# Another order of the attention and feed-forward stages in the second layer of a fused transformer kernel

## The chip, the core and the metric

One core of a Trainium2 chip. TensorE (PE) multiplies, its weight loads (PEld) overlap with its products; VectorE (DVE), ScalarE (ACT) and GpSimd (POOL) work element by element; SyncE (SP) issues the DMAs. The metric is the time of one execution on the device in microseconds; lower is better. A measurement here is the median of three executions.

## What is computed

A causal single-head attention with residual and layer norm (the front), then a block of two transformer layers with windowed attention, then a last residual and layer norm. Cut to what matters, for 8 sequences of 1024 tokens and 256 channels:

```python
x = layernorm(x + attn(x))                    # front: one head, causal
y = x
for l in range(2):                            # DEPTH
    h = shift_token(y)                        # second half of the channels from the token before
    q, k, v = split(h @ wqkv[l])              # 8 heads of 64
    q, k = rotary(l2norm(q) * qs[l], l2norm(k) * ks[l])
    # windows of 128 tokens: each looks at itself and the one before
    o = softmax(mask(8 * q @ k.T)) @ v
    y = y + o @ wo[l]
    h = layernorm(shift_token(y)) * lg[l] + lb[l]
    a, g = split(h @ w1[l] + b1[l])           # 682 hidden
    y = y + (a * gelu(g)) @ w2[l] + b2[l]
x = layernorm(x + y)
```

All of it is float32. Weight products run as three products of fp32r halves (high x high, high x low, low x high), which the helper `products` lists.

## The kernel before

`fronts` computes the front for all sequences and leaves x in DRAM (`x0_d`). `layers` then does both layers; the first leaves its result in `x1_d`. The unit of work is a window of 128 tokens; a pair of windows (256 tokens) shares one transposed input and one pass of the feed-forward. There are 2 x 8 x 8 = 128 windows and 64 pairs, 32 pairs for each layer.

The stages of a window, in `attention`:

- `prep` (once for a pair): load x, transpose it on PE (`l_xp`), write high and low halves (`l_xT`)
- `qk` (t, k), k = 0, 1: six products of 512 columns into `l_pqk`, which hold q and k of four heads; squares on ACT and sums on DVE (`l_ss`, L757), two products with the rotary tables on DVE (`l_t`, L764), two sums on POOL (L771)
- `v`: six products of 512 columns (`l_pv`), copied by ACT to `l_v`
- `unit`: inverse norms with POOL's power (L142, L144), and k scaled by them (L782)
- `turn` (t, k): four transpositions (`l_t` on PE), high half by ACT, low half by DVE into `ring`, which keeps three windows
- `sc` (w, u), u = 0, 1: scores of four heads, 12 products over 64 rows each; mask and row minimum on DVE (L843), exp on ACT (L703) into `l_e`. With u = 1 come the reciprocals of the sums (`rd`, L855), their transposition, a way through DRAM (`rd_d`, L860) and back spread over the partitions (`l_R`, L866)
- `et` (w, u): eight transpositions of `l_e` on PE, two ACT copies to `l_eT` (L885). Window 0 of a sequence has four, since it has no window before it
- `val` (w, u): 16 value products, each to 64 of the output's partitions, into one `l_po` per window
- `out`: `l_po` times `l_R` on DVE (`l_on`, L909), high half by ACT (L914), low half by POOL (L915)
- `proj`: 12 products with `wo` (`l_py`), added to x by DVE (L927). After an odd window the pair's feed-forward is put in a queue.

The feed-forward is a generator of 11 steps, one for each `side`: (1) the shifted copy `m_sh` by DMA (L947, L948), statistics on DVE (L152, L153), POOL's power (L144), `m_hn` on DVE (L964); (2) four transpositions `m_hp` and the halves `m_hT`; (3 to 8) `m_pag` for six chunks of the hidden size, 12 products of 256 columns, six for the last chunk, with gelu on ACT (L703), bias and product on DVE (L1013), halves by DVE (L1016) and POOL (L1017); (9, 10) `m_pf`, 17 products each; (11) the sum on DVE (L1043), in the second layer also the last norm (`o_st`, `o_mv`, L1052), and the store.

The order is written out by hand. `ORDER` is one round, for windows w and w + 1 with w = 2j; an entry such as `("sc", -2, 0)` means the stage `sc` of window w - 2 with u = 0. There are 11 `side` entries in a round, one pass of the feed-forward. The framework's scheduler puts the instructions into each engine's queue by priority and readiness. For PE the order is bound further by `queued` (a group's products are those with `part=True`, scores and values): all other products ahead of a group in the program come before it, and all behind it after it. Within a queue an instruction that waits holds up what stands behind it.

PSUM has eight banks: four `ps` buffers for everything but scores, and four `sc` buffers. In SBUF `l_eT` and `l_oT` have two buffers each, `l_v` four, `l_t` six, `x` six. `table` keeps ACT's exp and gelu from being mixed, since either needs its own table to be loaded.

Of the kernel before, what the change touches and what calls it, by code (L numbers as in the profile page):

```python
# [26 lines left out]
def kernel(  # L27
# [141 lines left out]
    for j, s in ((0, 1), (1, -1), (2, 1)):  # L169
        nc.gpsimd.affine_select(  # L170
            out=mask[:, j, :], in_=mask[:, j, :], compare_op=ALU.is_ge, fill=FAR,
# [38 lines left out]
    def q4(shape, name, dt):  # L210
        return qpool.tile(shape, dt, tag="q4", name=name, bufs=QB)

# [270 lines left out]
    def load_qkv(l, stage, W):  # L483

        wqk = pair([P, 2, 2, 2, INNER // 2], "wqk", wpool)
        wvv = pair([P, 2, INNER], "wvv", wpool)
        for c in range(2):
            for k in range(3):
                st = stage([P, INNER], f"st_qkv_{l}_{c}_{k}")
                nc.sync.dma_start(  # L490
                    out=st, in_=wqkv[l, c * P : (c + 1) * P, k * INNER : (k + 1) * INNER]
                )
                if k < 2:
                    s3 = st.rearrange("p (g f) -> p g f", g=2)
                    split_weight(wqk[0][:, c, :, k, :], wqk[1][:, c, :, k, :], s3)
                else:
                    split_weight(wvv[0][:, c, :], wvv[1][:, c, :], st)
                yield
        W["wqk"] = [t.rearrange("p c g k f -> p c (g k f)") for t in wqk]
        W["wv"] = wvv  # L500

    def load_wo(l, stage, W):
        W["wo"] = pair([P, INNER // P, E], "wo", wpool)
        for c in range(0, INNER // P, 2):
            st = stage([P, 2, E], f"st_wo_{l}_{c}")
            nc.sync.dma_start(
                out=st, in_=wo[l, c * P : (c + 2) * P, :].rearrange("(c p) e -> p c e", p=P)
            )
            split_weight(W["wo"][0][:, c : c + 2, :], W["wo"][1][:, c : c + 2, :], st)
            yield  # L510
# [52 lines left out]
    def load_b1(l, stage, ps, W):  # L563
        b1_tiles(l, W)
        for c in range(2):
            pb = ps(f"pb1_{l}_{c}")
            for k, m0, m1, st in w1_parts(l, stage, c):
                b1_part(W, pb, c, k, m0, m1, st)
            b1_add(W, pb)
            yield  # L570
# [37 lines left out]
    def load_w2(l, stage, W):  # L608
# [23 lines left out]
        yield  # L632

    QB = 4
    PSB = {"ps": 4, "sc": 4}
    ORDER = [
        ("qk", 0, 0), ("unit", -2), ("unit", -1), ("side", 1), ("turn", -2, 0), ("side", 1),
# [3 lines left out]
        ("v", 0), ("side", 1), ("prep", 2), ("v", 1), ("et", -2, 1), ("et", -1, 0),  # L641
        ("val", -2, 0), ("val", -2, 1), ("et", -1, 1), ("side", 1), ("qk", 1, 1),
        ("val", -1, 0), ("val", -1, 1), ("side", 1), ("side", 1), ("side", 1),
    ]

    def layers(pool, psum):
# [14 lines left out]
        def ps(name):  # L661
            return psum.tile([P, 512], FP, tag="ps", name=name, bufs=PSB["ps"])

        def ps_sc(name):
            return psum.tile([P, 2, 256], FP, tag="sc", name=name, bufs=PSB["sc"])

# [393 lines left out]
        def side(n):  # L1060
            for _ in range(n):
                if not queue:
                    return
                try:
                    next(queue[0])
                except StopIteration:
                    queue.pop(0)
# [3 lines left out]
        def run(name, w, *args):  # L1071

            if not 0 <= w < DEPTH * B * NT:
                return
            l, b, t = w // (B * NT), w // NT % B, w % NT
            if (l, b) not in A:
                if "wqk" not in Ws[l]:
                    for _ in load_qkv(l, stage, Ws[l]):
                        pass
                W = Ws[l]  # L1080

                def finished(p, xt):
                    queue.append(feed_forward(l, b, p, xt, W))

                A[l, b] = attention(l, b, W, finished)
            A[l, b][name](t // 2 if name == "prep" else t, *args)
            if name == "proj" and b == B - 1 and t == NT - 1 and l + 1 < DEPTH:
                for _ in load_wo(l + 1, stage, Ws[l + 1]):
                    pass
# [6 lines left out]
        later = chain(  # L1096
            *[load_b1(l, stage, ps, Ws.setdefault(l, {})) for l in range(1, DEPTH)]
        )
        for j in range(PAIRS + 3):
            w = 2 * j  # L1100
            if j >= 1:
                next(later, None)
            for item in ORDER:
                if item[0] == "side":
                    side(item[1])
                else:
                    run(item[0], w + item[1], *item[2:])
        while queue:
            side(1)

# [5 lines left out]
    with tc.tile_pool(name="lpool", bufs=1) as lpool, tc.tile_pool(  # L1116
        name="lpsum", bufs=1, space=PSUM
    ) as lpsum:
        layers(lpool, lpsum)
# [57 lines left out]
```

## Time and profile before

| | us |
|---|---|
| runs: median (lowest to highest of 3) | 2683.63 (2682.82 to 2688.84) |
| profiled execution: time | 2688.53 |
| its span, first to last instruction | 2686.7 |
| start of the first scores (`l_sc`) in the trace | 295.2 |
| first scores to first scores, rounds in the middle of layer 1 | 36.9; 35.1 where a sequence starts |
| the same in layer 2 | 37.5; 36.3 where a sequence starts |
| rounds across the change of layers (from 1457.5 and 1496.5) | 39.0 and 44.1 |
| mean granted TensorE clock | 0.986 |

The page cuts the span into 40 slices; the digits are tenths of the slice in which the engine was busy, `PEclk` is the granted clock:

```profile
PE   7998899999999999999999999999999999999997
PEld 5776799999999999999988888988888988889887
DVE  5787677777777777777778878887787877787775
ACT  5676466666666666666676666666666666666653
POOL 4565566666666666666666776676766767667673
PEclk8999899999999999999999999999999999999998
```

The first four slices or so are the front, then come layer 1 up to about slice 21 and layer 2. PE counts as busy from the issue of a product to its modelled end, so a full row does not say that there is nothing between products: the starts of the products in the timeline tell that. In the groups of the page a line can be that of a helper (L130, L133 and L91 stand for many places), so tiles are read, not lines.

### The profile page before, as it was taken

How to read it: one execution, taken by the hardware profiler on the slowest of the kernel's cores; microseconds unless marked ns; L12 is line 12 of the kernel's file. 1: busy time of each engine (PE TensorE's matmuls, PEld its weight loads, DVE VectorE, ACT ScalarE, POOL GpSimd, SP SyncE). 2: the span in 40 equal slices, each digit the busy share in tenths (PEclk: the TensorE clock that was granted, in tenths of full speed). 3: DMA queues.
4: the chain of work that ended last, by engine and by line, in shares of the span. 5: the costliest groups of instructions: out<-in, count | busy, mean ns of one | idle time of the engine just before them, and what ended most of it. 6: DMA issues, size and time to landing. Idle time of an engine off the chain costs nothing.

```text
span 2686.7 us, 61674 instructions
## 1 busy us (share of the span) xinstructions
PE 2615.7 (97%) x22336; PEld 2330.3 (87%) x22336; DVE 2059.4 (77%) x6304; ACT 1721.2 (64%) x4486; POOL 1743.0 (65%) x1996
## 2 busy tenths in 40 slices
PE   7998899999999999999999999999999999999997
PEld 5776799999999999999988888988888988889887
DVE  5787677777777777777778878887787877787775
ACT  5676466666666666666676666666666666666653
POOL 4565566666666666666666776676766767667673
PEclk8999899999999999999999999999999999999998
DMA  6332211111111111111121211111111111111110
GB/s 180 99 95 72 75 35 45 45 43 41 39 35 45 45 43 42 41 33 43 45 63 51 67 52 51 41 43 50 52 50 45 39 50 52 51 44 43 47 45 25
DMA packets 147265, 141.12 MB, mean 53 GB/s; under 512 B 28808, under 2 KB 123408, under 8 KB 146960
## 3 DMA queue, kind: packets, MB, share of 16 engines
q1 hardware_dynamic: 145600, 136.72, 17.4%
q8 instruction: 176, 2.88, 0.5%
q14 instruction: 129, 1.06, 0.1%
q10 hardware_dynamic: 1360, 0.46, 0.1%
HBM read 96.74 MB, written 27.81 MB: 46 GB/s over the span
## 4 chain that ended last, share of the span: by engine, by line
PE 65%; DVE 15%; POOL 8%; ACT 6%; issue 3%; DMA 2%; SPq 0%; POOLq 0%; DVEq 0%; ACTq 0%
PE m_pag L130 16%; PE l_pqk L130 10%; PE l_po L130 8%; PE l_et L133 6%; PE m_pf L130 6%; PE l_sc L130 4%; PE l_py L130 4%; PE l_pv L130 3%; ACT l_e L703 3%; PE l_t L133 3%; DVE l_t L764 2%; POOL l_t L771 2%; DVE l_ss L757 2%; DVE ring L91 2%; POOL l_oT L915 1%
## 5 line engine op out<-in xcount | busy, mean ns | idle before, releaser
L703 ACT ACTIVATE l_e<-l_sc,l_nm 128x256 f32<-128x256 f32 (+1 forms) x992 | 456.9, 481 | 216.8 <-DVE o_mv L153 107.7
L130 PE MATMUL m_pag<-m_hT,w_h 128*128 128x256 f32 (+1 forms) x2816 | 529.4, 288 | 0.7 <-ACT m_hT L90 0.7
L771 POOL TENSOR_TENSOR l_t<-l_t,l_t 128x256 f32<-128x256 f32 x512 | 369.8, 743 | 241.5 <-DVE l_t L764 241.5
L843 DVE CUSTOM_DVE_ANT_0 l_sc<-l_sc,mask,l_nrm_y 128x256 f32<-128x256 f32 (+1 forms) x1024 | 429.1, 466 | 45.8 <-ACT l_e L703 36.9
L130 PEld LDWEIGHTS m_pag<-m_hT,w_h 128*128 128x128 f32 (+1 forms) x2816 | 433.6, 188 | 17.7 <-issue 10.6
L703 ACT ACTIVATE m_gl<-m_pag,b 128x256 f32<-128x256 f32 (+1 forms) x384 | 181.9, 474 | 348.6 <-PE m_pag L130 348.5
L130 PE MATMUL m_pag<-m_hT,w_l 128*128 128x256 f32 (+1 forms) x1408 | 395.9, 281 | 0.0
L130 PE MATMUL l_pqk<-wqk_h,l_xT 128*128 128x512 f32 x1024 | 381.7, 414 | 1.4 <-ACT l_xT L90 0.8
L144 POOL TENSOR_TENSOR l_nrm_y<-l_nrm_a,half 128x16 f32<-128x16 f32 x128 | 373.6, 2918 | 10.5
L885 ACT COPY l_eT<-l_et 128x512 f32<-128x512 f32 (+1 forms) x512 | 274.5, 565 | 144.2 <-PE l_po L130 91.4
L764 DVE TENSOR_TENSOR l_t<-l_pqk,l_tab 128x512 f32<-128x512 f32 x512 | 327.3, 681 | 0.0
L1013 DVE SCALAR_TENSOR_TENSOR m_gl<-m_pag,b,m_gl 128x256 f32<-128x256 f32 (+1 forms) x384 | 183.6, 478 | 130.2 <-ACT m_gl L703 129.9
L133 PE MATMUL l_et<-ident,l_e 128*128 128x128 f32 x1920 | 266.3, 281 | 12.6 <-DVE l_cx L733 5.4
L1017 POOL TENSOR_TENSOR m_a<-m_gl,m_a 128x256 fp32r<-128x256 f32 x320 | 233.2, 735 | 54.3 <-DVE m_a L1016 53.0
L130 PEld LDWEIGHTS m_pag<-m_hT,w_l 128*128 128x128 f32 (+1 forms) x1408 | 264.0, 188 | 0.0
L133 PEld LDWEIGHTS l_et<-ident,l_e 128*128 128x128 f32 x1920 | 211.4, 141 | 58.6 <-DVE l_cx L733 12.5
L130 PE MATMUL m_pf<-w_h,m_a 128*128 128x256 f32 x1280 | 250.3, 282 | 0.0
L757 DVE TENSOR_REDUCE l_ss<-l_sq 128x8 f32<-128x512 f32 x256 | 175.1, 684 | 86.5 <-ACT l_sq L754 82.8
L130 PE MATMUL l_po<-l_eT,l_v 128*64 128x128 f32 x3840 | 239.5, 277 | 0.0
L130 PEld LDWEIGHTS l_po<-l_eT,l_v 128*64 128x64 f32 x3840 | 208.4, 137 | 34.1 <-issue 14.1
L142 POOL TENSOR_SCALAR l_nrm_a<-l_ss 128x16 f32<-128x16 f32 x128 | 32.3, 252 | 305.2 <-DVE l_ss L757 303.7
L130 PEld LDWEIGHTS l_pqk<-wqk_h,l_xT 128*128 128x128 f32 x1024 | 194.9, 190 | 38.1 <-DVE l_on L909 1.5
(168 smaller groups left out, 6704.8 us busy)
## 6 DMA issues: line engine op xcount, KB each, us to landing
l_R<-rd_d SPq DMA_DIRECT2D x256, 128.0 KB
x<-x_d SPq DMA_DIRECT2D x96, 256.0 KB
l_tab<-tab_d SPq DMA_DIRECT2D x128, 128.0 KB
xin<-in_L_attn_x_dram SPq DMA_DIRECT2D x16, 512.0 KB
x_d<-xin SPq DMA_DIRECT2D x16, 512.0 KB
rd_d<-l_rT SPq DMA_DIRECT2D x512, 1.0 KB
x_d<-x SPq DMA_DIRECT2D x32, 256.0 KB
out_dram<-x SPq DMA_DIRECT2D x32, 256.0 KB
```

Source lines behind the costliest of these rows:

```text
L91: nc.vector.tensor_tensor(lo, src, hi.bitcast(FP), ALU.subtract)
L130: queued(nc.tensor.matmul(*args, **kw), part)
L133: queued(nc.tensor.transpose(*args), False)
L144: nc.gpsimd.tensor_tensor(r, a, half.to_broadcast([P, n]), ALU.pow)
L703: ins = nc.scalar.activation(*args, **kw)
L757: nc.vector.tensor_reduce(st["ss", t][:, k * HEADS : (k + 1) * HEADS], sq.rearrange("p (g d) -> p g d", d=DH), AX.X, ALU.add)
L764: nc.vector.tensor_tensor(tt[j].rearrange("p (k h d) -> p k h d", k=2, d=DH), p3, tb.unsqueeze(2).to_broadcast([P, 2, HEADS // 2, DH]), AL ...
L771: nc.gpsimd.tensor_add(a[:, :, s, :], a[:, :, s, :], bsw[:, :, 1 - s, :])
L843: nc.vector.tensor_tensor_reduce(dst, dst, mk, st["nrm", w][:, 8 * u + h : 8 * u + h + 1], BIG, ALU.add, ALU.min, nm[:, one],)
L885: nc.scalar.copy(eT[:, j, 0:m], pt[:, 0:m])
L1013: nc.vector.scalar_tensor_tensor(gl[0:z, :], a_ps, W["b1"][0:z, 0, m : m + 1], gl[0:z, :], ALU.add, ALU.mult)
L1017: nc.gpsimd.tensor_tensor(a[1], gl[0:z, :], a[0].bitcast(FP), ALU.subtract)
```

## The change

Up to round 32 `ORDER` is followed as before. From round 33 (w = 66, while window 64 is the first of the second layer) rounds follow `ORDER_1`. In it the values of window w - 3 come directly after the scores of w - 2, and those of w - 2 directly after the scores of w - 1; `et`, `out` and `proj` are at other windows and places. Before the first such round, two rounds of `ORDER_1` are gone through without `side`, in which only those stages run that have not run before (`done` keeps them), and two steps of the feed-forward are taken. Stages, tiles, buffers and weights are as before.

```diff
+    SWITCH, CATCH = 33, 2
     PSB = {"ps": 4, "sc": 4}
     ORDER = [
         ("qk", 0, 0), ("unit", -2), ("unit", -1), ("side", 1), ("turn", -2, 0), ("side", 1),
...
         ("v", 0), ("side", 1), ("prep", 2), ("v", 1), ("et", -2, 1), ("et", -1, 0),
         ("val", -2, 0), ("val", -2, 1), ("et", -1, 1), ("side", 1), ("qk", 1, 1),
         ("val", -1, 0), ("val", -1, 1), ("side", 1), ("side", 1), ("side", 1),
     ]
+    ORDER_1 = [
+        ("side", 1), ("unit", -2), ("turn", -2, 0), ("turn", -2, 1), ("unit", -1), ("qk", 0, 0),
+        ("et", -3, 1), ("side", 1), ("et", -3, 0), ("sc", -2, 0), ("sc", -2, 1), ("val", -3, 0),
+        ("val", -3, 1), ("side", 1), ("qk", 0, 1), ("out", -3), ("turn", -1, 0), ("side", 1),
+        ("side", 1), ("proj", -3), ("turn", -1, 1), ("et", -2, 1), ("prep", 2), ("et", -2, 0),
+        ("v", 0), ("side", 1), ("qk", 1, 0), ("v", 1), ("side", 1), ("sc", -1, 0),
+        ("sc", -1, 1), ("val", -2, 0), ("val", -2, 1), ("side", 1), ("side", 1), ("side", 1),
+        ("side", 1), ("out", -2), ("qk", 1, 1), ("proj", -2),
+    ]
...
+        done = set()
+
+        def one_round(order, w, sides):
+            for item in order:
+                if item[0] == "side":
+                    if sides:
+                        side(item[1])
+                    continue
+                stage = (item[0], w + item[1], *item[2:])
+                if stage not in done:
+                    done.add(stage)
+                    run(*stage)
+
         for j in range(PAIRS + 3):
             w = 2 * j
             if j >= 1:
                 next(later, None)
-            for item in ORDER:
-                if item[0] == "side":
-                    side(item[1])
-                else:
-                    run(item[0], w + item[1], *item[2:])
+            if j < SWITCH:
+                one_round(ORDER, w, True)
+                continue
+            if j == SWITCH:
+
+                for back in (4, 2):
+                    one_round(ORDER_1, w - back, False)
+                side(CATCH)
+            one_round(ORDER_1, w, True)
         while queue:
             side(1)
```

## The prediction

> **What bounds it now.** I read the busy time per engine first, then single rounds of the loop cut out as stretches, then TensorE (PE) and VectorE (DVE) in order of time, then what the weight loads waited for. The time of the profiled execution is 2688.53 us (span 2686.7); the median shown is 2683.63, 4.9 us less, and I carry differences over to it unchanged.
>
> The page's first part, and three stretches from one round's first score matmul to the next (length, busy time and instructions per engine, clock, DMA share, GB/s): a round of layer 1, a round of layer 2, and the layer-2 round in which a sequence starts.
>
> ```profile
> PE 2615.7 (97%) x22336; PEld 2330.3 (87%) x22336; DVE 2059.4 (77%) x6304; ACT 1721.2 (64%) x4486; POOL 1743.0 (65%) x1996
> ```
> ```profile
> 905.98:942.89 36.91, 36.91 (x330) 33.75 (x329) 28.30 (x86) 24.46 (x63) 23.65 (x28) 1.00 0.14 41
> 2247.14:2284.68 37.54, 37.52 (x330) 33.77 (x329) 29.45 (x92) 24.43 (x63) 25.80 (x31) 1.00 0.17 47
> 2359.68:2395.97 36.29, 35.78 (x306) 31.97 (x305) 29.34 (x92) 22.87 (x63) 25.89 (x32) 1.00 0.18 49
> ```
>
> PE issues 330 matmuls in either layer, so TensorE's queue sets the round; what can be won is time between its instructions. Layer 2 takes 0.60 us more in 24 of its 32 rounds and (36.28 against 35.11) 1.17 us more in the 8 in which a sequence starts: 24 x 0.60 + 8 x 1.17 = 23.8 us. PE in order of time (start, us, operation, count) shows where, first layer 1, then layer 2:
>
> ```profile
> 921.81 0.60 PE L133 MATMUL l_xp<-ident,x 128*128 128x128 f32 x4
> 922.16 0.47 PE L130 MATMUL l_pv<-wvv_h,l_xT 128*128 128x512 f32 x1
> ...
> 923.63 1.93 PE L133 MATMUL l_et<-ident,l_e 128*128 128x128 f32 x16
> 925.49 1.97 PE L130 MATMUL l_po<-l_eT,l_v 128*64 128x128 f32 x32
> ```
> ```profile
> 2262.93 0.60 PE L133 MATMUL l_xp<-ident,x 128*128 128x128 f32 x4
> 2263.45 0.50 PE L130 MATMUL l_pv<-wvv_h,l_xT 128*128 128x512 f32 x1
> ...
> 2264.95 2.37 PE L133 MATMUL l_et<-ident,l_e 128*128 128x128 f32 x16
> 2267.25 1.97 PE L130 MATMUL l_po<-l_eT,l_v 128*64 128x128 f32 x32
> 2269.15 1.09 PE L133 MATMUL l_et<-ident,l_e 128*128 128x128 f32 x8
> ...
> 2271.74 0.40 PE L130 MATMUL l_pqk<-wqk_h,l_xT 128*128 128x512 f32 x1
> 2272.06 1.97 PE L130 MATMUL l_po<-l_eT,l_v 128*64 128x128 f32 x32
> 2273.96 0.50 PE L130 MATMUL m_pag<-m_hT,w_h 128*128 128x256 f32 x2
> 2274.30 0.28 PE L130 MATMUL m_pag<-m_hT,w_l 128*128 128x256 f32 x1
> ```
>
> From `l_xp` to the next start is 0.35 in layer 1 and 0.52 in layer 2; `l_et` x16 takes 1.86 and 2.30. The weight loads of that layer-2 round name the reason, DVE readers of the four `ps` buffers that come late:
>
> ```profile
> PEld l_et L133 <- DVE l_cx L733: 0.2, 1, 0.2
> PEld l_et L133 <- DVE l_t L764: 0.2, 1, 0.2
> PEld l_pv L130 <- DVE x L927: 0.2, 1, 0.2
> ```
>
> The other loss is at the half-array products. The `l_pqk` before `l_po` holds PE 0.32 us instead of 0.23, the first two `m_pag` after it 0.34 instead of 0.23. I took eight start-to-start slots around each such boundary between 400 and 2600 us and subtracted the steady slots (transposition 109 ns, pair of half-array score products 118, pair of value products 107, 256-column product 118, 512-column 232). Medians in ns: transposition to scores 199, product to scores 195, scores to transposition 150, transposition to values 171, product to values 155, values to transposition 162, values to product 207.
>
> **The change: boundaries.** No instruction or DMA is added or removed; PE's order moves, and what the other queues get when. A round of `ORDER` has four half-array groups: 199 + 150 (scores of w-2), 195 + 150 (scores of w-1), 171 + 162 and 155 + 207 (values) = 1389 ns. `ORDER_1` has two, each entered from transpositions and left to a feed-forward product: 2 x (199 + 207) = 812 ns, plus twice scores to values, which the trace doesn't contain. Bounds: 0 if nothing happens between the two, 150 + 171 = 321 if an exit and an entry are both paid. I take 160, the nearest row (product to values 155, transposition to values 171). The round then pays 1132, a saving of 0.26 us (0.58 to -0.07), over 32 rounds 8 us (18 to -2).
>
> The Trainium skill, "TensorEngine Tiling (Array Packing)", section "Tiling Modes", says that a change of tiling mode, not just of tile, drains TensorE. Scores use half the rows and values half the columns, so by the rule the new boundary is itself a drain and the saving is about 0.26 us; without it 0.58.
>
> **Buffers.** In `ORDER` the copies into `l_eT` (2 buffers) of w-1 wait for w-2's values, and `l_po` of two windows stays in `ps` through some 15 us. In `ORDER_1` each window's values leave before the next window's transpositions, and `out` follows 3.4 us (PE work) after one pair of values and 5.7 after the other. I walked the four `ps` buffers through the new round with the rows' durations (ACT copy 0.6, DVE low part 0.6, `l_ss` and both `l_t` 1.9 together): none is missing by over 0.2 us. I count the 0.60 and 1.17 us as removed. ACT still changes between exp and gelu once each way per round. `out` to `proj` (DVE 0.68, ACT 0.62, POOL 1.3) has at least 5.9 us of PE work beside it, and the transposed scores' copies have the 1.6 us of scores. SP's queue gets the same loads.
>
> **The new wait.** What comes short is the feed-forward's first step: last projection, `x` on DVE (L927), the shifted copy by DMA, statistics, POOL's power, `m_hn`, and then `m_hp` on PE, the last free product ahead of the next scores, which may not pass it. DVE in the same layer-2 round:
>
> ```profile
> 2262.98 0.42 DVE L927 TENSOR_TENSOR x<-l_py,x 128x256 f32<-128x256 f32 x1
> ...
> 2266.55 0.49 DVE L152 BATCH_NORM_STATS2 m_st<-m_sh 128x6 f32<-128x128 f32 x2 [0.31 <-DMA m_sh<-x]
> ...
> 2268.51 0.35 DVE L964 TENSOR_SCALAR m_hn<-x,m_mv,m_rs_y 128x128 f32<-128x128 f32 x1 [1.14 <-POOL m_rs_y L144]
> ...
> 2269.28 0.34 DVE L964 TENSOR_SCALAR m_hn<-m_sh,m_mv,m_rs_y 128x128 f32<-128x128 f32 x1
> ```
>
> PE leaves the projection at 2261.53, so `m_hn` ends 8.1 us later, because L927 starts 1.44 us late. In layer 1, where it starts 0.34 late, the median end is 6.83. Now `m_hp` starts 8.54 us after the projection, so nothing waits. In `ORDER_1` there lie between them 24 transpositions (2.62) and three 512-column stages (3 x 1.40): 6.82, with `m_hp`'s own 0.40 7.22. `m_hp` can't end before `m_hn` plus 0.19 (0.08 from release to start, one slot), so PE waits for whatever `m_hn` exceeds 7.03. How late is L927? The feed-forward's last half now ends 1.40 us ahead of the projection. DVE then has `l_ss` and `l_t` of qk (w, 1) until 16.1 us of the round, a ring low part to 16.7, L1043 to 17.4, two `o_st` to 18.0, while the projection ends at 17.2: 0.8 late. So `m_hn` ends at 6.83 + 0.46 = 7.29 and PE waits 0.26 us; where a sequence's window 0 has 8 transpositions less (0.87), 1.13.
>
> **Sum.** Ordinary round -0.26 - 0.60 + 0.26 = -0.60; the round with window 0 -0.26 - 1.17 + 1.13 = -0.30. 24 x 0.60 + 8 x 0.30 = 16.8 us. In the last rounds, with no new windows, less work covers `m_hp`: 20 transpositions (2.2 us) instead of 6.8, a wait of 4.8 where today about 2.6 are lost: +2. Between the layers (the rounds at 1457 and 1497 take 39.0 and 44.1 us for the weights) I expect the same loss, +-4. Net -14.8: 2673.7 for the profiled execution, **2669** for the median.
>
> **Rivals.**
> - *The shifted copy comes late and PE waits at `m_hp` in every round (slower).* It decides from `m_hn` ending 7.75 us after the projection, where the wait of 0.72 eats all of the gain (32 x 0.72 = 23, the sum without this wait). For it: layer 2 today ends at 8.1, a wait of 1.07, +11 us: 2695. If POOL's 3.2 us for a window's norm (252 + 2918 ns) lie half in front of it, another 51: 2746. Against it: L927's lateness today comes from DVE work around the final norm that is placed elsewhere.
> - *Gelu behind exp (slower).* Four `m_pag` now follow [scores, values] at once, and their gelus stand behind eight exps (3.7 us) and a table load (1.28). By my walk the first `m_pag` buffer comes back 1.5 us before the qk product needs it. From there each us is 32 us: 2701 at one us more.
> - *Nothing to be seen.* A scheduler orders PE's queue; it could undo the order, or the waits move to other buffers. Against the first: today's PE sequence is `ORDER`'s, stage for stage, in the rounds read. 2684.
> - *More than forecast*: no wait at `m_hp` beyond window 0's and scores to values for nothing: 2669 - 8 - 10 = 2651.
>
> **Chances.** Forecast with its better end 0.56 (2651 to 2678), late `m_hp` 0.24, gelu 0.08, nothing 0.12. 0.2% is 5.4 us, about what a measurement can tell from no change. Faster 0.58, same 0.12, slower 0.30. The range goes from 2651 to 2704, which takes in the mild form of both slower cases.
>
> **What would show it.** Right: two half-array groups per layer-2 round, scores to values at 0.1 to 0.2 us, rounds near 36.9, `m_hp` with waits of 0.2 to 0.3. Wrong: rounds over 37.5 with PE idle before `m_hp` named after `m_hn` or POOL's power, idle before `m_pag` or `l_pqk` named after gelu, or the first layer's rounds changed from 36.9.

## The result and the profile after

The changed kernel takes 2694.91 us (median of 6 runs, 2691.72 to 2701.59), the kernel before 2683.40 beside it (6 runs, 2681.60 to 2688.84): ratio 1.0042, 95% interval 1.0031 to 1.0054. It is 0.42% slower. 2669 and "faster" had been forecast; the time lies inside the range. That it is near the 2695 of the mild form of the first rival is coincidence: that form has `m_hp` waiting 1.07 us in every round, which the trace does not show.

The page's first part for the kernel after; its time is 2692.83 us, its span 2691.0.

```profile
PE 2601.4 (97%) x22336; PEld 2330.2 (87%) x22336; DVE 2068.4 (77%) x6304; ACT 1725.2 (64%) x4486; POOL 1739.2 (65%) x1996
```

PE's count is the same and its busy time 14.3 us less, yet the span is longer: PE waits more. From here on lines inside `layers` are 10 higher (L927 is L937, L964 is L974). Three layer-2 rounds of the kernel after as stretches, columns as before: an ordinary one, one with a sequence's window 0, and a third, again ordinary.

```profile
1989.20:2026.13 36.93, 36.90 (x329) 33.88 (x328) 29.73 (x92) 24.42 (x63) 25.59 (x31) 1.00 0.15 48
2361.86:2398.57 36.71, 35.68 (x305) 32.08 (x304) 29.10 (x92) 22.97 (x63) 25.66 (x32) 1.00 0.16 48
2138.03:2176.29 38.26, 37.52 (x329) 33.88 (x328) 29.57 (x92) 24.42 (x63) 25.65 (x31) 1.00 0.15 47
```

The first has the length of the forecast round: 37.52 - 0.60 = 36.92. The second was to be 35.98; it is 36.71, against 36.29 before. The third has the same work as the first and takes 1.33 us more. Before, ordinary rounds of layer 2 lay between 37.45 and 37.53; now seven of them take 37.2 to 38.3, and two of those with window 0 take 37.4 and 38.0.

PE in order of time in the kernel after, at one of the new boundaries (start, us, operation, count):

```profile
2045.67 0.28 PE L130 MATMUL l_sc<-ring 64*128 64x256 f32 x2
2045.79 0.40 PE L130 MATMUL l_sc<-ring,ring 64*128 64x256 f32 x4
2046.12 1.97 PE L130 MATMUL l_po<-l_eT,l_v 128*64 128x128 f32 x32
2048.01 0.50 PE L130 MATMUL m_pag<-m_hT,w_h 128*128 128x256 f32 x2
```

Values follow scores with nothing between. Four score products issued every 118/2 = 59 ns would end their slots at 2045.79 + 0.24; the values start at 2046.12. Over 60 such places, with the reckoning of the prediction, scores to values costs 154 ns (median; 148 to 162 from the 10th to the 90th percentile). 160 was taken. This agrees with the rule that the prediction quoted from the Trainium skill, "TensorEngine Tiling (Array Packing)", section "Tiling Modes": the change from half the rows to half the columns costs about what the other boundaries cost (150 to 207 ns).

So the order does what it says. A round is counted by the loop's j, from its first scores to the next round's. To see where the gain went, I put the time from the first `l_pqk` to the last product together from steady slots (same work, 2238.1 and 2238.2 us), the boundaries at their medians, and the rest, which is waiting:

| boundaries + waits, us | rounds to 29 | 30-34 | 35-60 | 61 to the end | sum |
|---|---|---|---|---|---|
| before | 40.0 + 22.9 | 6.9 + 14.6 | 35.9 + 24.0 | 5.5 + 19.0 | 168.8 |
| after | 40.0 + 22.3 | 6.2 + 22.8 | 29.1 + 29.0 | 4.9 + 22.1 | 176.4 |

Boundaries: 8.1 us less, as forecast. Waits: 15.7 us more, of which 8.2 lie where the order changes, 5.0 in the steady rounds, 3.1 at the end. (In one profiled execution each. These two are 7.6 us apart here, the medians 11.5, and one order need not take the same time twice: in experiments 1 and 6 rounds 30-34, still in the old order, have about 2.3 us less of waits than the kernel before has here. Where the rest of the 11.5 lies is not shown.)

What the weight loads waited for in the kernel after, 1590 to 2585 us (us in total, times, longest):

```profile
PEld l_pqk L130 <- DVE m_gl L1023: 8.1, 13, 0.8
...
PEld m_hp L133 <- DVE m_hn L974: 3.8, 9, 1.1
...
PEld l_t L133 <- ACT m_gl L713: 3.1, 7, 0.5
PEld l_pv L130 <- DVE ring L91: 2.5, 7, 0.4
PEld l_et L133 <- ACT l_eT L895: 2.2, 7, 0.3
```

The readers that held the buffers before (`l_cx` 9.6 us, `l_t` 5.7 in this window) are gone, as forecast. But waits have come as well. By the reckoning of the table an ordinary round of layer 2 had 1.39 us of boundaries and 0.79 of waits before, and an undisturbed one now has 1.12 and 0.48; an ordinary round of layer 1 before had 0.2 of waits. So the waits fell by 0.3, not by 0.60. Some 0.3 us of new ones stand in the first round above, two of them these:

```profile
PEld l_t L133 <- issue: 0.2, 1, 0.2
PEld m_pf L130 <- DVE l_nm L853: 0.2, 1, 0.2
```

In place of the old readers stand the chain from exp over the table load and gelu to the `l_pqk` that needs the first `m_pag` buffer, and `m_hp`. In the round with window 0 alone `l_pqk` waits 0.8 and `l_t` 0.5: its value products are 0.9 us shorter, so the four `m_pag` come sooner, while the exps (of a whole window) do not; this is read from the order and the waits, no run tested it.

**The third round.** DVE in order of time in the kernel after, first a round without the delay, then this one:

```profile
2112.21 0.42 DVE L937 TENSOR_TENSOR x<-l_py,x 128x256 f32<-128x256 f32 x1
...
2115.54 0.48 DVE L152 BATCH_NORM_STATS2 m_st<-m_sh 128x6 f32<-128x128 f32 x2
...
2118.38 0.34 DVE L974 TENSOR_SCALAR m_hn<-m_sh,m_mv,m_rs_y 128x128 f32<-128x128 f32 x1
```
```profile
2149.13 0.42 DVE L937 TENSOR_TENSOR x<-l_py,x 128x256 f32<-128x256 f32 x1
...
2153.89 0.49 DVE L152 BATCH_NORM_STATS2 m_st<-m_sh 128x6 f32<-128x128 f32 x2 [1.48 <-DMA m_sh<-x]
...
2156.60 0.34 DVE L974 TENSOR_SCALAR m_hn<-m_sh,m_mv,m_rs_y 128x128 f32<-128x128 f32 x1
```

From the sum to the statistics of the shifted half it takes 3.33 us in the one and 4.76 in the other, with DVE idle for 1.48 and waiting for the copy. DMA queues in the stretch from the sum to the landing (packets, MB, share), first of the round without the delay, then of the late one:

```profile
q1 hardware_dynamic: 476, 0.33, 36.9%
```
```profile
q1 hardware_dynamic: 431, 0.26, 21.7%
q8 instruction: 1, 0.02, 1.3%
q14 instruction: 1, 0.01, 0.6%
```

One packet of 16384 bytes of instructions lies in the late copy. Packet by packet it occupies a DMA engine from 2151.79 to 2152.72, and two packets of 512 bytes, by their place the copy's last, go at 2152.70 to 2152.83, some 0.7 us later after the sum than the copy's last packets in the rounds without the delay. (The reading follows 1.06 us behind them in place of some 0.4; what this remainder is isn't shown.) Such a packet comes every 15.1 us on average and takes 1.05 us (median of 176). In the steady rounds of the kernel after, every landing later than 4.0 us after the projection (7 rounds) has one in it.

What it costs here: the copy is read 1.4 us late and `m_hn` ends 1.3 late (7.5 us after the sum in place of 6.2). `m_hp` starts 0.5 beyond its place and waits for the rest within its group, and then the `l_pqk` behind the gelu waits too. The weight loads of the late round:

```profile
PEld m_hp L133 <- issue: 0.7, 1, 0.7
PEld l_pqk L130 <- DVE m_gl L1023: 0.4, 1, 0.4
PEld m_hp L133 <- DVE m_hn L974: 0.3, 1, 0.3
```

### The profile page after: what moved, and what is told of

It reads as the page before. It is cut to its first block, busy times and chain, and to the rows that moved or that the text cites. A ratio compares the mean times of both kernels' runs of the same rounds, so it can differ in the third digit from the quotient of the medians.

```text
span 2691.0 us, 61542 instructions
## 1 busy us (share of the span) xinstructions
PE 2601.4 (97%) x22336; PEld 2330.2 (87%) x22336; DVE 2068.4 (77%) x6304; ACT 1725.2 (64%) x4486; POOL 1739.2 (65%) x1996
## 3 DMA queue, kind: packets, MB, share of 16 engines
q14 instruction: 128, 1.05, 0.1%
## 4 chain that ended last, share of the span: by engine, by line
PE 79%; DVE 8%; ACT 6%; POOL 3%; DMA 2%; issue 1%; SPq 0%; POOLq 0%; DVEq 0%; ACTq 0%
PE m_pag L130 15%; PE l_pqk L130 12%; PE m_pf L130 10%; PE l_po L130 8%; PE l_et L133 7%; PE l_sc L130 7%; PE l_py L130 6%; PE l_pv L130 5%; PE l_t L133 4%; ACT l_e L713 2%; DMA m_sh<-x 1%; DVE l_t L774 1%; PE f_sc L130 1%; PE m_hp L133 1%; PE f_pz L395 1%
## 5 line engine op out<-in xcount | busy, mean ns | idle before, releaser
L130 PEld LDWEIGHTS m_pag<-m_hT,w_h 128*128 128x128 f32 (+1 forms) x2816 | 431.3, 187 | 15.1 <-issue 10.1
L713 ACT ACTIVATE m_gl<-m_pag,b 128x256 f32<-128x256 f32 (+1 forms) x384 | 175.2, 474 | 284.7 <-PE m_pag L130 243.6
L925 POOL TENSOR_TENSOR l_oT<-l_on,l_oT 128x512 fp32r<-128x512 f32 x128 | 165.1, 1289 | 262.2 <-ACT l_oT L924 262.2
L895 ACT COPY l_eT<-l_et 128x512 f32<-128x512 f32 (+1 forms) x512 | 268.6, 568 | 70.8 <-PE l_po L130 40.8
L133 PE MATMUL l_et<-ident,l_e 128*128 128x128 f32 x1920 | 257.5, 278 | 4.9 <-ACT l_v L802 1.6
L130 PE MATMUL m_pf<-w_h,m_a 128*128 128x256 f32 x1280 | 256.1, 286 | 0.0
```

Of the source, the lines that this page charges most:

```text
L130: queued(nc.tensor.matmul(*args, **kw), part)
L133: queued(nc.tensor.transpose(*args), False)
L713: ins = nc.scalar.activation(*args, **kw)
L895: nc.scalar.copy(eT[:, j, 0:m], pt[:, 0:m])
L925: nc.gpsimd.tensor_tensor(oT[1], on, oT[0].bitcast(FP), ALU.subtract)
```

## The experiments

The theories moved on with the runs; each expectation says what they were at the time. The kernel before was timed again with every batch.

**1. Is it the loading of weights that makes the change-over dear?** First batch, kernel before 2684.41 us.

```diff
-    SWITCH, CATCH = 33, 2
+    SWITCH, CATCH = 36, 2
```

> ORDER_1 starts at round 36 instead of 33, after the second layer's weights are in place. Theory A (the loss at the change of layers comes from ORDER_1's shorter distances meeting the weights' loading; in the trace of the changed kernel the rounds 30 to 34 hold 8.2 us more waits than before): 2694.9 - 7 = about 2687 us, and rounds 31 to 33 as long as in the kernel before (37.4, 39.0, 44.1 us). Rival B (any change from one order to the other costs this much, wherever it lies): about 2694, with the 8 us now in rounds 34 to 37.

2695.05 us (2689.26 to 2697.21), ratio 1.0037 (1.0025 to 1.0050). Rounds 32 to 34 (31 to 33 in the expectation's count) took 37.30, 37.26 and 43.71 and the change-over, now clear of the weights, 40.50 and 41.10, some 7 us over the usual two rounds. So the weights are not the cause. In the round after SWITCH (1578 to 1621 us) the weight loads waited for:

```profile
PEld m_hp L133 <- issue: 4.7, 1, 4.7
PEld l_et L133 <- ACT ring L90: 1.1, 1, 1.1
```

In that round `et`(-3) and `val`(-3) fall away, having been done by the old order. By the slots that is 3.8 us of PE work (16 transpositions, 32 value products, their boundaries; the 5.6 in a later expectation is too high), while DVE and POOL have a full round, and `m_hp` arrives before `m_hn` (PE's own row has it idle for 4.28 us until `m_hn`). The missing work doesn't lie between the projection (left at 1586.21) and `m_hp`: the usual 6.9 us stand there. It is `m_hn` that ends 13.2 us after the projection in place of 6.7, and DVE shows how:

```profile
1588.16 0.41 DVE L937 TENSOR_TENSOR x<-l_py,x 128x256 f32<-128x256 f32 x1
...
1593.75 0.69 DVE L767 TENSOR_REDUCE l_ss<-l_sq 128x8 f32<-128x512 f32 x1 [2.77 <-ACT l_sq L764]
1594.35 1.28 DVE L774 TENSOR_TENSOR l_t<-l_pqk,l_tab 128x512 f32<-128x512 f32 x2
1595.55 0.48 DVE L152 BATCH_NORM_STATS2 m_st<-m_sh 128x6 f32<-128x128 f32 x2
...
1598.26 0.35 DVE L974 TENSOR_SCALAR m_hn<-x,m_mv,m_rs_y 128x128 f32<-128x128 f32 x1 [1.99 <-POOL m_rs_y L144]
```

The sum starts 1.9 us after the projection. In DVE's queue `l_ss` and `l_t` of the next qk stand ahead of the statistics, and wait 2.77 us for ACT's squares; in the ordinary round from 2112.21 they come behind `m_hn` (2118.64). In SP's queue a part of the reciprocals' way through DRAM stands between the two copies, and the second is issued 3.9 us after the sum (1592.08) in place of 1.2. So the order of the other engines' queues in this round has its part in the price, beside the missing work of PE; no run separates the two.

**2. qk ahead of the four `m_pag`**, to take it out of the gelu's way.

```diff
-... ("val", -2, 1), ("side", 1), ("side", 1), ("side", 1), ("side", 1), ("out", -2), ("qk", 1, 1), ("proj", -2),
+... ("val", -2, 1), ("qk", 1, 1), ("side", 1), ("side", 1), ("side", 1), ("side", 1), ("out", -2), ("proj", -2),
```

> In ORDER_1 the stage qk (w+1, 1) comes directly after the values, ahead of the four feed-forward steps instead of behind them. Theory A (those four m_pag stand behind the exps and the table load, and l_pqk waits 0.6 to 0.8 us for a buffer that a gelu holds, 13 times in the second layer, 8 us by the weight loads' waits): the wait of l_pqk for m_gl falls to under 2 us in all, 2694.9 - 6 = about 2689. Rival B (the wait is only handed to the next stage that needs a buffer, l_py or m_pag): 2693 to 2697 with the same sum of waits under another name.

2696.10 us (2686.97 to 2697.70), ratio 1.0039 (1.0025 to 1.0053): nothing won. Its weight loads, 1590 to 2585 us:

```profile
PEld l_pqk L130 <- DVE m_gl L1023: 10.0, 27, 0.9
PEld m_pag L130 <- ACT m_gl L713: 7.8, 20, 0.6
```

In either order some product waits for a buffer that a gelu holds; here two kinds do, where in the kernel after it was mostly `l_pqk`.

**3. `m_hp` behind the scores and values**, with qk early as in 2, to give the normalization 3.5 us.

```diff
-... ("side", 1), ("sc", -1, 0), ("sc", -1, 1), ("val", -2, 0), ("val", -2, 1), ("side", 1), ...
+... ("sc", -1, 0), ("sc", -1, 1), ("val", -2, 0), ("val", -2, 1), ("side", 1), ("qk", 1, 1), ("side", 1), ...
```

> As in the run with qk early, and the feed-forward's second step (m_hp) comes after the scores and values of w-1 and w-2 instead of ahead of them, so that 3.5 us more of TensorE work lie between the projection and m_hp. Theory A (m_hp waits for m_hn whenever the shifted copy lands over 0.2 us late, in the steady rounds, at the change of layers (4.2 and 2.3 us) and near the end (4.5 us), and all that waits for scores behind it): waits at m_hp under 2 us but for the last window pair, 2694.9 - 6 (gelu) - 3 (steady) - 8 (change and end) = about 2678, under the kernel before. Rival B (m_hT's halves now stand behind the exps on ACT and the row minima on DVE, and the first m_pag waits instead): m_pag idle by 0.5 us or more in each round, 2695 to 2710.

2737.57 us (2729.08 to 2744.37), ratio 1.0201 (1.0185 to 1.0217). `m_hp` no longer waits for `m_hn`, but `m_hT`'s high half is ACT's, and ACT is then in the exps. Same window:

```profile
PEld m_pag L130 <- ACT m_hT L90: 44.1, 26, 2.6
PEld m_pag L130 <- DVE m_hT L91: 14.0, 26, 0.8
```

This is why `m_hp` stands ahead of the scores: its copy must reach ACT before the exps do.

**4. The new order from the first layer on**, which doubles the rounds that gain.

```diff
-    SWITCH, CATCH = 33, 2
+    SWITCH, CATCH = 1, 2
```

> ORDER_1 from round 1, so that the first layer has it too. Theory A (the boundaries give 0.26 us a round in either layer, and the rounds in which a sequence starts give it back by 1.5 us or so through waits at l_et, l_pqk and l_t): ordinary rounds of layer 1 36.6 to 36.8 instead of 36.9, sequence starts 36.2 to 36.7 instead of 35.1; 2694.9 - 24 x 0.2 + 8 x 1.4 = about 2701. Rival B (the waits come from the second layer's additional work on DVE and POOL, for the final norm and x0): sequence starts in layer 1 stay near 35, 2694.9 - 8 = about 2687.

2729.62 us (median of 5, one of them 4260.32, the others 2723.32 to 2735.52), ratio 1.0168 (1.0151 to 1.0184), worse than either forecast. Boundaries in the rounds to 29 fall from 40.0 to 32.3 us as they should; waits rise from 22.9 to 55.3. Its weight loads in layer 1 (400 to 1350 us) name the same three places as layer 2 does:

```profile
PEld l_pqk L130 <- DVE m_gl L1023: 8.6, 17, 0.8
PEld l_t L133 <- ACT m_gl L713: 8.3, 18, 0.5
PEld m_hp L133 <- DVE m_hn L974: 8.1, 17, 1.8
```

**5. The projection earlier.** Second batch, kernel before 2685.39 us.

```diff
-        ... ("out", -3), ("turn", -1, 0), ("side", 1), ("side", 1), ("proj", -3), ("turn", -1, 1), ("et", -2, 1), ...
+        ... ("out", -3), ("turn", -1, 0), ("turn", -1, 1), ("proj", -3), ("side", 1), ("side", 1), ("et", -2, 1), ...
```

> Only ORDER_1 is edited: turn(-1,1) and proj(-3) come ahead of the two sides that stood before them, so that the normalization of the pair (y add, shifted copy, statistics, power, four m_hn) begins about 1.7 us earlier against m_hp, which in the changed kernel follows it with no slack. Theory A (in the rounds of the second layer the changed kernel loses time where the shifted copy lands late: 7 of 28 rounds, 34, 36, 40, 47, 49, 51 and a little 53, in which a 16384-byte instruction packet of about 1 us lies in the copy, and each gives 0.6 to 1.3 us): m_hp no longer waits for m_hn, these rounds fall from 37.7-38.3 to 36.9, total 2687 to 2690; the rounds at a sequence's start keep their wait of l_pqk for the gelu. Rival B (the slack is taken from the operand of the projection instead, whose POOL subtraction ends 1.38 us before the projection now): l_py waits for l_oT 0.1 to 0.5 us in every round, total 2693 to 2700.

(The rounds that the expectation lists are 36, 38, 42, 49, 51, 53 and 55 in the count used here.) 3008.57 us (3005.39 to 3013.47), ratio 1.1208 (1.1190 to 1.1226). This run tells nothing on the theory: I had overlooked how `side` counts. CATCH 2 leaves one of round 33's eleven sides with an empty queue; with the projection ahead of the sides it finds the new feed-forward there, and from then on every step comes one `side` early. `m_hp` stands ahead of qk (1, 0), and PE waits for it (1590 to 2585 us):

```profile
PEld m_hp L133 <- issue: 87.5, 33, 4.7
PEld l_pqk L130 <- DVE m_gl L1023: 21.5, 21, 1.8
```

It does show that PE waits out a late `m_hn` in full: 3.5 to 4 us in a round. A further kernel had the same edit, with v (1) moved behind the values:

> The edit of the earlier projection, and besides v(1) comes behind side 2 (m_hp), scores(-1) and values(-2), so that exps, table load and gelu begin 1.4 us earlier against qk(1,1), which waits for the first m_pag buffer. Theory A (both chains of the last part of the round, normalization to m_hp and exps to gelu to qk, lack slack, and nothing else does): the l_pqk wait for m_gl (8.1 us in rounds 34 to 61) falls under 1 us, l_t's for m_gl too, m_hp waits only in the rounds of a late copy; steady rounds 36.7 to 36.9 and 35.9 to 36.3 at a sequence's start, total 2679 to 2686. Rival B (the wait is handed on: the values then wait for their transposed exps or l_pv's buffer is held by its copy behind the exps): m_pag or l_po waits 0.3 us or more in most rounds, total 2690 to 2700.

It shares the fault: 3043.05 us, ratio 1.1336 (1.1316 to 1.1355).

**6. A late change-over.**

```diff
-    SWITCH, CATCH = 33, 2
+    SWITCH, CATCH = 62, 2
```

> SWITCH 33 to 62: 28 rounds fewer in the new order, all else as changed. Theory A (the loss is the filling and emptying of a pipeline that is one stage deeper, about 8 us in the rounds of the change-over, whose TensorE work has been done ahead, and 3 us at the end; the rounds between give 8 us of boundaries and take 5 of waits): the change-over costs its 8 us here as well, total 2692 to 2698, and rounds 62 and 63 show the idle TensorE that rounds 31 to 35 show now. Rival B (the loss grows with the number of rounds in the new order): total 2683 to 2686, near the kernel before.

2694.11 us (2692.07 to 2695.94), ratio 1.0035 (1.0022 to 1.0047), as theory A has it. With all steady rounds in the old order the loss is the same. Rounds 35-60 have the waits of the kernel before (35.9 + 24.4), the rounds from 61 on 5.0 + 29.8 against 5.5 + 19.0: 10.3 us more. The weight loads of the round after SWITCH (2557 to 2600 us):

```profile
PEld m_hp L133 <- issue: 4.7, 1, 4.7
PEld l_sc L130 <- issue: 0.5, 2, 0.3
```

It is the wait of experiment 1, to a tenth of a microsecond, at another time of the program.

**7. The normalization without the copy.** The statistics and `m_hn` take the second half of the columns from x itself, so the shift in the feed-forward's input is left out; the copies still run.

```diff
-            mean_rstd(sm, [x1[:, i, 0:P], sh[:, i, :]], mv, i, f"{nm0}_st{i}")
+            mean_rstd(sm, [x1[:, i, 0:P], x1[:, i, P:E]], mv, i, f"{nm0}_st{i}")
...
-                for c, src in ((0, x1[:, i, 0:P]), (1, sh[:, i, :])):
+                for c, src in ((0, x1[:, i, 0:P]), (1, x1[:, i, P:E])):
```

> The order is the changed one. The normalization and its statistics take columns 128 to 255 from x itself and no longer from the tile that the shifted copy fills (the copies still run, nobody reads them): what is computed is therefore not the reference's shifted input. The chain y add to m_hn then holds no DMA. Theory A (late copies cost the second layer's rounds about 6 us): m_hn ends some 2.5 us earlier, m_hp never waits for it in rounds 35 to 61, total 2686 to 2690, and what is left over the kernel before is the change-over and the end. Rival B (late copies are covered and the gelu behind the exps is what the rounds lose by, with or without them): rounds as in the changed kernel, total 2693 to 2697.

2682.96 us (12 runs, 2679.13 to 2687.06), ratio 0.9993 (0.9980 to 1.0005): 0.49% below the changed kernel by the two ratios, more than expected, and level with the kernel before. That is no like-for-like comparison: the edit takes the wait for the copy out of both layers and of the last rounds, and the kernel before was not run without it. Every ordinary round from the 35th to the 61st now takes 37.08 to 37.14 and every one with window 0 36.61 or 36.62: the scatter is gone. Boundaries and waits against the kernel after: 27.2 for 29.0 in the change-over, 53.9 for 58.1 in rounds 35-60, 20.9 for 27.0 at the end, where `m_hp` had waited some 4.4 and 6.0 us; the second of these stands in the kernel before as well (6.2). Weight loads, 1590 to 2585 us:

```profile
PEld l_t L133 <- ACT m_gl L713: 8.2, 20, 0.5
PEld l_pqk L130 <- DVE m_gl L1023: 4.1, 7, 0.6
```

`m_hp` no longer waits for `m_hn`; the seven waits of `l_pqk` are the rounds with window 0, and `l_t` waits for a gelu in all others. So even without the copy, ordinary rounds stay 0.2 us above the best of the changed kernel.

**8. The projection earlier, done properly**: ahead of the second `m_pf` group, which is held behind it, with CATCH 1 to keep the steps in place. Third batch, kernel before 2685.61 us.

```diff
-    SWITCH, CATCH = 33, 2
+    SWITCH, CATCH = 33, 1
...
-        ... ("turn", -1, 0), ("side", 1), ("side", 1), ("proj", -3), ("turn", -1, 1), ("et", -2, 1), ("prep", 2), ...
+        ... ("turn", -1, 0), ("turn", -1, 1), ("prep", 2), ("proj", -3), ("side", 1), ("side", 1), ("et", -2, 1), ...
...
-                passes(py[:, i * E : (i + 1) * E], steps)
+                passes(py[:, i * E : (i + 1) * E], steps, group["py"] if i else None)
```

> ORDER_1 with turn(-1,1), prep(2) and proj(-3) ahead of the second m_pf group (17 products, 2.1 us), the m_pf group held behind the projection by an order of issue, and CATCH 1, which keeps the feed-forward's steps at the places that they have in the changed kernel. Between the projection and m_hp then lie about 8.0 us of TensorE work in place of 6.9: 1.1 us of slack for the normalization. Theory A (no slack there is what lets the late shifted copies cost time): m_hp no longer waits in rounds 35 to 60, their waits fall from 29.0 us to 24 to 26, total 2686 to 2691. Rival B (the slack is paid elsewhere: l_et(-2,1) and l_et(-2,0) now stand back to back and wait for the copies of ACT, as the 16 transpositions of the kernel before did, 0.3 to 0.7 us a round): total 2694 to 2706.

2772.11 us (2766.78 to 2773.07), ratio 1.0308 (1.0292 to 1.0324). Rival B in kind, at another place than it named. Weight loads, 1590 to 2585 us (lines 2 to 5 higher):

```profile
PEld l_xp L135 <- issue: 49.6, 25, 2.0
PEld l_t L135 <- ACT m_gl L717: 15.8, 25, 0.7
```

`l_xp` now follows two `l_t` directly, behind the first `m_pf` and `l_pqk`: five tiles for four `ps` buffers, and the `l_t` are read by ACT after its exps. PE stands 1.8 us there. What ended it is DVE's `l_t` (L778), the last reader of the `l_pqk` buffer: in the two rounds read it ends 0.10 us before `l_xp` starts (1879.76 and 1879.86, 1919.16 and 1919.26). DVE had stood 1.2 us ahead of it for `l_sq`, which ACT takes up after the exps. `m_hp`'s wait for `m_hn` falls from 3.8 to 2.4 us in this window, and the slack costs far more than that.

**9. A full first round.** Round 35 leaves out `et`(-1) and `val`(-1), which the new order then does as its own.

```diff
-    SWITCH, CATCH = 33, 2
+    SWITCH, CATCH = 36, 2
...
+                short = [i for i in ORDER if i[:2] not in (("et", -1), ("val", -1))]
-                one_round(ORDER, w, True)
+                one_round(ORDER if j < SWITCH - 1 else short, w, True)
```

> SWITCH 36 as in the earlier run, and round 35, the last in the old order, leaves et(-1) and val(-1) to round 36, which does them as its et(-3) and val(-3): the round that is lighter by a window's value products is now one of the old order, and the first of the new order is a full one. Theory A (the change-over costs its 7 to 8 us because in the first round of ORDER_1 the normalization is reached with too little TensorE work between; a full first round has that work): the excess of the rounds 34 to 37 over their usual times falls from 7 us to 3 or less, total 2687 to 2691. Rival B (a round that is lighter for TensorE alone cannot be shorter, since the other engines and the chains through them keep their length, wherever it is put): round 35 takes its 37 us although 5.6 us of matmuls are gone, total 2693 to 2697.

2693.35 us (12 runs, 2688.59 to 2699.52), ratio 1.0025 (1.0015 to 1.0035). The two rounds take 43.42 and 38.30, together 81.7, against 40.50 and 41.10, 81.6, in experiment 1. As rival B has it, the lighter round isn't shorter by what it lacks, in either of the two places; the ratio's interval overlaps that of experiment 1. With both edits of 8 and 9:

> The two edits together (projection ahead of the second m_pf group, et(-1) and val(-1) left out of round 35, SWITCH 36, CATCH 1). Theory A (their gains add, since one acts in the change-over and the other in steady rounds): total 2680 to 2687, the kernel before or a little less. Rival B (one of them gives its gain back): total 2690 to 2700.

2766.15 us, ratio 1.0288 (1.0270 to 1.0307): the gain of 0.2% over experiment 8 is within the intervals.

**10. The same saving without the deeper pipeline.** Fourth batch, kernel before 2686.24 us.

```diff
-    SWITCH, CATCH = 33, 2
+    SWITCH, CATCH = 99, 2
...
-        ... ("v", 1), ("et", -2, 1), ("et", -1, 0), ("val", -2, 0), ("val", -2, 1), ("et", -1, 1), ("side", 1), ("qk", 1, 1), ("val", -1, 0), ("val", -1, 1), ...
+        ... ("et", -2, 1), ("v", 1), ("qk", 1, 1), ("et", -1, 0), ("et", -1, 1), ("side", 1), ("val", -2, 0), ("val", -2, 1), ("val", -1, 0), ("val", -1, 1), ...
...
-            "sq": 4, "t": 6, "v": 4, "eT": 2, ... "sh": 3,
+            "sq": 2, "t": 6, "v": 4, "eT": 4, ... "sh": 2,
```

> The order of the kernel before in all rounds (SWITCH 99: ORDER_1 is never used), in which only the last third is arranged anew: et(-2,1), v(1), qk(1,1), et(-1,0), et(-1,1), side 1 (m_hp), then val(-2) and val(-1) one behind the other. This saves the same kind of boundary as the change (a round leaves and enters the value products once less: 162 + 155 = 317 ns by the medians of the profile before, 19 to 20 us over 62 rounds), with no stage more of depth, so with no change-over, and m_hp stays 7.3 us behind the projection, m_hn being ready after 6.7. It needs four l_eT buffers in place of two, paid with l_sq 4 to 2 and m_sh 3 to 2. Theory A (what made the changed kernel slower is the deeper pipeline and the missing slack, not the merging of groups): total 2664 to 2676, faster than both kernels. Rival B (transpositions in one run wait for their copies on ACT, 2.4 us of them against 2.9 us of copies, and m_hp for a late copy: 0.3 to 0.6 us a round): total 2680 to 2700.

2755.25 us (2755.07 to 2763.78), ratio 1.0264 (1.0247 to 1.0281). Boundaries fall by 19.6 us, from 88.3 to 68.7, exactly as worked out; waits rise from 80.5 to 169.3. Weight loads, 1590 to 2585 us:

```profile
PEld l_pv L130 <- DVE l_t L774: 24.4, 25, 1.0
PEld l_et L133 <- ACT l_eT L895: 12.0, 22, 0.6
PEld m_hp L133 <- ACT l_eT L895: 8.5, 20, 0.4
```

Rival B, and larger: the second window's v waits in nearly every round for a `ps` buffer that DVE's `l_t` of the previous qk frees. That the smaller `l_sq` and `m_sh` rings had a part in it was not tried. No version is faster than the kernel before.

## Why the prediction failed, step by step

- **Boundaries, -0.26 us a round: right.** 35.9 to 29.1 in 26 rounds is 0.26 each, 8.1 us in all. Scores to values is 154 ns.
- **Buffers, the 0.60 and 1.17 us gone: right for the readers that it named, too large as a term.** New waits of about 0.3 us a round came, so that ordinary rounds gained 0.3 by it, not 0.60. Undisturbed ordinary rounds take 36.91 to 37.00 and 36.92 was forecast, but that is luck: these waits are as long as the wait at `m_hp` of the next point, which did not come.
- **L927 0.8 us late, `m_hn` 7.29 after the projection, 0.26 of waiting: wrong in both terms.** The sum starts 0.20 after the projection in all rounds but the change-over's and the last, `m_hn` ends 6.70 after it, and `m_hp` goes at 6.9 without a wait. The walk had two `o_st` ahead of the sum; in the trace they come behind it (2112.55 after 2112.21).
- **The copy as a fixed duration: the step that failed in the ordinary rounds.** I took its landing from medians, though the slack was nil. With an instruction packet in it, it lands up to 1.5 us later; seven steady rounds pay 0.4 to 1.3 us each for that, 6.7 in all. In the old order the sum starts 1.4 late in layer 2, the copy is read 5.0 us after the projection, DVE having waited 0.3 for it, and `m_hp` goes at 8.5 in ordinary rounds, so that a reading at 5.0 costs nothing there. The trace before had the late copies too: in six of rounds 2 to 31 it was read 4.6 to 5.0 us after the projection, where the median is 3.7. Experiment 7 took the dependence away and the scatter with it.
- **Gelu, "comes back 1.5 us before the qk product needs it": wrong where a sequence starts.** In rounds with window 0 it comes 0.8 late, and `l_t` 0.5 late behind it. I walked the buffers through an ordinary round only and in the window-0 round took only the `m_hp` path, where the shorter transpositions showed; that the shorter values bring the `m_pag` forward I did not see. Forecast -0.30 for such a round, measured +0.38: 0.68 x 7 = 4.8 us. The price of a late copy is also larger by it: in the third round above `l_pqk` waits 0.4 us for a gelu on top of the wait at `m_hp`.
- **Between the layers "the same loss, +-4", tail +2: the step that failed by most.** No price was put on entering and leaving the deeper order. The change-over costs 8.2 us of waits and the end 3.1, against 0 and 2. The new order carries values, `out` and `proj` a stage later. Entering it means one round that is light for PE and full for the others, leaving it means a tail with work left over; experiment 1 paid it three rounds later, 6 with 29 fewer rounds in the new order, 9 spread over the previous round, at 1.0025 to 1.0037.

From -14.8: +9 for change-over and end, +5 for the window-0 rounds, +7 for late copies give about +6, against the +7.6 of the two profiles (168.8 to 176.4).

Of the rivals the first was right about the mechanism, a late shifted copy and a wait at `m_hp`, but in one round of four, not in all, and for another reason; the second was right about the place and wrong about its condition, since it needs no slower exps. Neither has the change-over, which alone takes as much (8.2 us) as the boundaries won (8.1). What isn't shown is why, in experiment 7, `l_t` still waits for a gelu in ordinary rounds.

## What to carry over

An order that removes stalls on a path at 97% is worth the stalls minus the slack it spends: list for each cross-engine chain the time to spare in the new order, and where it is nil, take the chain's worst duration in the trace, not its median. Changing to this deeper schedule in mid-run had an entry and an exit price, a wait of a whole chain each time, to be set against the gain per round times the rounds left; here 8 us of gain over 32 rounds met 10 to 11. Moving products earlier or later traded the wait for another each time (for one of the four PSUM buffers in experiments 2, 8 and 10, for ACT's copy behind the exps in 3), so buffers and copies must be walked through the unusual rounds (first window, first and last round) as well.

## What was unexpected in the hardware

Instruction packets go with late small copies. Over five kernels in the new order (after, and experiments 1, 2, 4 and 9), rounds 35 to 61, from 38 on in experiments 1 and 9, 129 rounds can be compared. In 37 of them a 16384-byte instruction packet starts 1.0 to 3.9 us after the projection, and the shifted copy is read at 4.35 us (median; over 4.2 in 27 of them, at most 5.41). In the 92 without one it is read at 3.61, and over 4.2 in two; in these two SP had issued the copy 1.1 and 1.5 us later than usual, behind `l_R` and `l_tab` in its queue. That the packet is the cause rests on this agreement and on the packet times; moving the packets was not tried. In the kernel before the 28 steady rounds of layer 2 had no such packet between the sum and the landing; why some rounds meet one was not worked out.
